# Constant row numbers, an earlier query and another bank for the keys in a four-layer graph network

## The chip, the core and the metric

The kernel runs on one core of one Trainium2 chip. The metric is device time in microseconds for one launch: 3656.0 us as the median of three runs of the kernel before (3653.54 to 3663.65). The profile below is of one profiled execution, whose span is 3611.7 us.

## What is computed

Four graph layers follow each other on x (4096 x 256) with one 4096 x 4096 adjacency of zeros and ones. Each layer ends with a residual and a layer norm. The reference, cut:

```python
# layer 0: mean over neighbours, then a linear layer
deg = adj.sum(1); agg = adj @ x / max(deg, 1); y = relu(concat([x, agg]) @ W + b)
# layer 1: two steps; R = row-normalised (adj + I), A = sparse attention
for n in range(2):
    q = Xa @ W1.T @ W2.T; k = Xa @ W3.T
    A = top_p(softmax(q @ k.T), 0.9)      # keep the largest until 0.9 of the mass, renormalise
    Xf = R @ Xf; Xa = A @ Xa
    Z = Z + Xf @ U1[n].T + Xa @ U2[n].T
y = layernorm(X + Z) * g + b
# layer 2: neighbours, and one number per node from the diagonal of adj @ adj
y = concat([x, adj @ x, diag(adj @ adj)]) @ weight + bias
# layer 3: symmetric normalisation with degree ** -0.5
y = relu((d[:, None] * (adj + I) * d[None, :]) @ x @ W + b)
```

## The kernel before

The 4096 rows are cut into NT = 32 tiles of 128 rows. The work is written as one stream for a framework that assigns the queues: each instruction belongs to a fixed engine, and the framework orders the instructions of an engine by their place in the program and by a model of when they are ready. An instruction can so stand in its engine's queue well ahead of the tile that it serves. All semaphores come from the framework. A tile of memory with `bufs=4` has four places in turn, and writing the fifth waits until the readers of the first are done. [...] `mm_bank` and `acc_bank` are one bank each, of which `half("mm")` and `half("acc")` hand out the two halves in turn.

**Layer 0** (12 to 485 us). `l0_main(it)` loads the adjacency of a tile in four pieces of 512 KB (L129, issued by GpSimd, four buffers), multiplies each with x in two fp32r halves (L160), casts each piece to bytes on ScalarE for later (L234), writes it to `adj8_d`, and adds it into `sums` on VectorE (L239 to L244). `l0_degrees(it-1)` makes from `sums` the degree, the reciprocals `rdeg` and `rs`, and `dinv`, the degree to the power −0.5, by one GpSimd instruction a tile (L259). `l0_end(it-1)` applies the linear layer (L274, into a half of `mm_bank`) and the layer norm. `l0_keys(it-2)` turns a finished row tile by TensorE (L170), copies it to SBUF as `xt` (L172, ScalarE), multiplies it with W3 into the other half of `mm_bank` (L201), and splits the result into an upper part (L194, `upk`, VectorE; L203, ScalarE) and a rest (L204, VectorE), which go to `kS`, the keys.

**Layer 1** has two steps. In each, iteration i of `run_step` works on three tiles at once: logits of tile i+2 in eight chunks (L358, copied out by L359), the choice of the largest entries of tile i+1 (cd), and the products of tile i. `pieces` runs through the eight chunks g = 0 to 7; after chunk g it calls the operations that `run_step` has registered with `at(g, f)`. The order of the work is thus the order of the `at` calls and their groups. Step 0 takes the 16 largest entries of a row: MAX8 over groups (L377), two FIND_INDEX8 (L474), gathers of rows by GpSimd (L616, 8 buffers G), diagonal weights (L701, `dg`), and matmuls (L703). Beside it run the product with adj (L632; adjacency bytes cast by L629) and, for the diagonal, L638. Step 1 keeps all entries above a threshold in place: MATCH_REPLACE8 (L602) and four masked products (L607) on VectorE, then transposes and matmuls over all chunks (L686, L711).

Rows that the choice can't settle are marked `bad`. `flag` counts them by two small matmuls (L536, L537), works out each row's place in a list (`slot` L542, `at` L543), writes the row numbers (`ids`, L544), and scatters the row numbers to those places in DRAM (L550, GpSimd, `list_d`). The places and row numbers are tiles of four buffers each. Late tiles of such rows are read back from the list (L801, L803) and done again.

`query` makes the query of tile i+3: it turns the rows (L170, L172), multiplies (L338, into a half of `mm_bank`), and splits the product like the keys (L194, L341 on ScalarE, L342 on VectorE). It is registered in group 6 in both steps. `mix` (L764, L766 for `h`, and in step 0 L772) multiplies the outcome of the tile before with U1 and U2, in groups 1 and 2, also by way of `mm_bank`.

**Layers 2 and 3** (3030 us to the end) are again products with the adjacency (L160) with linear layers and norms. `dinv` is used there first.

Of the kernel before, what the change touches and what calls it, by code (L numbers as in the profile page):

```python
# [12 lines left out]
I32 = mybir.dt.int32  # L13
# [35 lines left out]
def gnn_stack(ctx, tc, x, adjt, adjn, w0, b0, w1, w2t, w3t, u1t, u2t, ln_g, ln_b, w2, b2, w3, b3, out):  # L49
# [114 lines left out]
    def transposed(*srcs):  # L164

        n = 2 * len(srcs)
        ps = ps_tr.tile([P, 4, P], F32, tag="tr", name="tr")
        for s, src in enumerate(srcs):
            for c in range(2):
                nc.tensor.transpose(ps[:, 2 * s + c, :], src[:, c * P : (c + 1) * P], ident)  # L170
        t = work.tile([P, 4, P], F32, tag="xt", name="xt")
        nc.scalar.copy(t[:, :n, :], ps[:, :n, :])  # L172
        return t
# [22 lines left out]

    def make_keys(xt, dst):

        ps = half("mm")
        for c in range(2):  # L200
            nc.tensor.matmul(ps[:, :P], w3t_sb[:, c, :], xt[:, c, :], start=(c == 0), stop=(c == 1))  # L201
        up = upper(ps[:, :P])
        nc.scalar.copy(dst[:DA, :], up[:DA, :])  # L203
        nc.vector.tensor_sub(dst[DA:, :], ps[DA:, :P], up[DA:, :])  # L204


    with tc.tile_pool(name="l0", bufs=1) as l0, tc.tile_pool(name="l0w", bufs=2) as l0w:
# [14 lines left out]
        for h in range(2):  # L222
            nc.scalar.dma_start(w3t_sb[:, :, h * DA : (h + 1) * DA], w3t.rearrange("(c p) o -> p c o", p=P))
        x1 = xpool.tile([P, NT, D], F32, tag="X", name="x1")

        def l0_main(it):
            acc = ps_acc.tile([P, 512], F32, tag=("acc", "nef")[it % 2], name="acc")
# [21 lines left out]
        def l0_degrees(it, sums):  # L249
            pd = half("acc")  # L250
            nc.tensor.matmul(pd[:, 0:1], sums[:, :P], ones_col, start=True, stop=True)
            deg = pd[:, 0:1]
            rd = work.tile([P, 1], F32, tag="rdeg", name="rdeg")
            nc.vector.tensor_scalar(rd, deg, 1.0, None, op0=ALU.max)
            nc.vector.reciprocal(rd, rd)
            d1 = work.tile([P, 1], F32, tag="deg1", name="deg1")
            nc.vector.tensor_scalar(d1, deg, 1.0, None, op0=ALU.add)
            nc.vector.reciprocal(rs[:, it : it + 1], d1)
            nc.gpsimd.tensor_tensor(dinv[:, it : it + 1], d1, mhalf, op=ALU.pow)  # L259
            return rd  # L260

        def l0_agg(acc, rd):
# [5 lines left out]
        def l0_end(it, agg):  # L268
            xi = l0w.tile([P, D], F32, tag="x0i", name="x0i")
            nc.scalar.dma_start(xi, rows(x, it))  # L270
            xt = transposed(xi, agg)
            ps = half("mm")
            for c in range(4):
                nc.tensor.matmul(ps, xt[:, c, :], w0_sb[:, c, :], start=(c == 0), stop=(c == 3))  # L274
# [12 lines left out]

        acc = None
        for it in range(NT + 2):
            if 1 <= it <= NT:  # L290
                agg = l0_agg(acc, l0_degrees(it - 1, sums))
            if it < NT:
                acc, sums = l0_main(it)
            if it >= 2:
                l0_keys(it - 2)
            if 1 <= it <= NT:
                l0_end(it - 1, agg)


    with tc.tile_pool(name="l1", bufs=1, reuse_waits="tile") as l1:  # L300
# [20 lines left out]
        nc.vector.memset(spare0, 0.0)  # L321
        blank = l1.tile([P, NT], I32, name="blank")
        nc.gpsimd.iota(blank, pattern=[[0, NT]], base=N, channel_multiplier=1)
        for t in list_d:
            nc.sync.dma_start(t[:N, :].rearrange("(k p) o -> p (k o)", p=P), blank)

# [3 lines left out]
                nc.scalar.dma_start(t, src[n].rearrange("(c p) o -> p c o", p=P))  # L330
                cur[name] = t

        def query(xi):

            xt = transposed(xi)
            ps = half("mm")
            for c in range(2):
                nc.tensor.matmul(ps[:, :P], wq_sb[:, c, :], xt[:, c, :], start=(c == 0), stop=(c == 1))  # L338
            up = upper(ps[:, :P])
            q = [work.tile([P, P], F32R, tag=f"q{k}", name=f"q{k}", bufs=3) for k in range(2)]  # L340
            nc.scalar.copy(q[0], up)  # L341
            nc.vector.tensor_sub(q[1], ps[:, :P], up)  # L342
            return q
# [182 lines left out]
        def flag(st):  # L526


            pb = half("mm")
            later = st.get("later")  # L530
            if later is None:
                nc.tensor.matmul(pb[:1, 0:1], st["bad"], ones_col, start=True, stop=True)
                st["nb"] = small("nbad", 1, I32)[:1, :]
                nc.scalar.copy(st["nb"], pb[:1, :1])
                return
            nc.tensor.matmul(pb[:, 0:1], ones_sq, st["bad"], start=True, stop=True)  # L536
            nc.tensor.matmul(pb[:, 1:2], before, st["bad"], start=True, stop=True)  # L537
            sofar, slot = small("sofar"), small("slot")
            nc.vector.tensor_add(sofar, later["base"], pb[:, 0:1])

            at, ids = small("at", 1, I32, 4), small("ids", 1, I32, 4)
            nc.vector.scalar_tensor_tensor(slot, pb[:, 1:2], later["base"], spare, op0=ALU.add, op1=ALU.subtract)  # L542
            nc.vector.scalar_tensor_tensor(at, slot, st["bad"], spare, op0=ALU.mult, op1=ALU.add)  # L543
            nc.vector.tensor_scalar(ids, spare, float(st["tile"] * P - N), None, op0=ALU.add)  # L544
            later["base"] = sofar
            if st["tile"] == NT - 1:

                st["to"] = to = small("to_last", 1, I32, 1)
                nc.vector.scalar_tensor_tensor(to, st["bad"], float(P), ids, op0=ALU.mult, op1=ALU.add)
            nc.gpsimd.indirect_dma_start(  # L550
                out=list_d[cur["n"]], out_offset=bass.IndirectOffsetOnAxis(ap=at[:, 0:1], axis=0), in_=ids, in_offset=None)

        def bit_by_bit(st):

# [302 lines left out]
        def run_step(n, es):  # L857
# [31 lines left out]
            for i in range(-2, NT):  # L889
# [18 lines left out]
                for g, fs in zip((1, 2), last):  # L908
                    for f in fs:
                        at(g, f)  # L910
                if cd is not None:
                    peak_groups(cd)
                    at(1, exp_rows, cd)
# [189 lines left out]
```

## The time and the profile before

| from the profile page | value |
|---|---|
| span | 3611.7 us |
| PE busy | 3114.6 us, 86% |
| PEld (weight loads) busy | 2528.6 us, 70% |
| DVE (VectorE) busy | 2364.5 us, 65% |
| ACT (ScalarE) busy | 1464.9 us, 41% |
| POOL (GpSimd) busy | 1005.1 us, 28% |
| mean granted TensorE clock | 0.935 |
| L544 `ids`, DVE, x64 | 9.3 us, 150 ns each |
| L259 `dinv`, POOL, x32 | 18.1 us, 566 ns each |
| scatter to `list_d`, issue to landing | 8.3 us median |
| gathers G, issue to landing | 4.4 us median |

A share of busy time is a mean over stages that have different limits, so the stages have to be read one by one. A matmul's end is modelled in the records, so a busy PE may still be slower than it could be: the granted clock, 1.0 or 0.5, says by how much. A wait is put down to what released it last; only waits of the engine that sets the end of its stage cost time.

### The profile page before, as it was taken

Reading aid. Unit: us, or ns where it says so; the run is one execution under the profiler, and the core shown is the slowest. Engines: PE = TensorE matmul, PEld = TensorE weight load, DVE = VectorE, ACT = ScalarE, POOL = GpSimd, SP = SyncE. Lnnn points to the kernel's source line nnn. Section 1 sums busy time; section 2 is a strip of 40 time slices with the busy share of each in tenths; the row PEclk is TensorE's granted clock in tenths of the full one; section 3 lists DMA queues with packets and bytes.
Section 4 is the critical chain, followed back from the end, with each engine's and each line's share of the span. In section 5 each row is a group of like instructions: output and inputs, shape, how many; then the busy total and the mean of one; then the engine's idle time right before and its main releaser. Section 6 shows DMA issues by size and latency. Waiting matters only on the chain. (4 is left out here: it accounts for less than half of the span.)

```text
span 3611.7 us, 46113 instructions
## 1 busy us (share of the span) xinstructions
PE 3114.6 (86%) x14780; PEld 2528.6 (70%) x14780; DVE 2364.5 (65%) x7144; ACT 1464.9 (41%) x2590; POOL 1005.1 (28%) x1328
## 2 busy tenths in 40 slices
PE   7777857898899899868898989999999737999998
PEld 5666645777777777646777777777788625887776
DVE  5566545776767777734688889799889673434333
ACT  3343334554545555444544545555465301111000
POOL 1222203666666666610000000100101012222332
PEclk8999978999999999988999999999999868999999
DMA  7777665676667767723000012011111007887887
GB/s 225 207 217 210 203 93 155 156 178 171 170 163 179 176 176 177 177 86 116 28 23 23 26 31 40 24 31 34 34 33 33 17 19 231 246 246 241 269 271 227
DMA packets 269343, 484.19 MB, mean 134 GB/s; under 512 B 44096, under 2 KB 186240, under 8 KB 269088
## 3 DMA queue, kind: packets, MB, share of 16 engines
q0 software_dynamic: 101760, 339.45, 34.5%
q1 hardware_dynamic: 150352, 125.73, 12.7%
q10 hardware_dynamic: 16976, 15.95, 1.5%
q8 instruction: 120, 1.97, 0.2%
q14 instruction: 135, 1.11, 0.1%
HBM read 423.45 MB, written 57.54 MB: 133 GB/s over the span
## 5 line engine op out<-in xcount | busy, mean ns | idle before, releaser
L632 PE MATMUL acc_r<-xh,adjq 128*128 128x512 f32 x2048 | 639.3, 444 | 49.1 <-ACT adjq L629 36.8
L616 POOL DMA_INDIRECT G<-x_d,cols x512 | 496.3, 969 | 355.1 <-PE acc_bank L703 262.9
L711 PE MATMUL acc_bank<-xa,at 128*128 128x256 f32 x2304 | 569.5, 387 | 18.0 <-ACT at L689 17.5
L160 PE MATMUL acc<-xh,adjt 128*128 128x512 f32 x2048 | 544.3, 416 | 45.4 <-DVE xh L137 29.4
L632 PEld LDWEIGHTS acc_r<-xh,adjq 128*128 128x128 f32 x2048 | 395.2, 199 | 152.8 <-ACT adjq L629 61.4
L358 PE MATMUL lg<-kS,q 128*128 128x512 f32 x1104 | 407.8, 456 | 97.7 <-ACT q L341 83.7
L160 PEld LDWEIGHTS acc<-xh,adjt 128*128 128x128 f32 x2048 | 391.8, 196 | 136.2 <-ACT xh L136 31.2
L711 PEld LDWEIGHTS acc_bank<-xa,at 128*128 128x128 f32 x2304 | 424.5, 194 | 80.1 <-ACT at L689 28.9
L629 ACT CAST adjq<-adj 128x512 fp32r<-128x512 uint8 x512 | 315.3, 619 | 387.3 <-issue 128.4
L377 DVE MAX8 cand<-e 128x8 f32<-128x256 f32 x1024 | 384.0, 415 | 40.1 <-ACT e L359 39.0
L129 POOL DMA_DIRECT2D adjt<-in_adjt x384 | 208.6, 544 | 695.4 <-PE acc L160 392.9
L359 ACT COPY e<-lg 128x512 f32<-128x512 f32 x552 | 317.8, 584 | 166.9 <-PE lg L358 164.8
L184 POOL TENSOR_TENSOR rstd<-ve,mhalf 128x1 f32<-128x1 f32 x168 | 102.7, 611 | 800.4 <-DVE ve L182 747.9
L703 PE MATMUL acc_bank<-G,dg 128*128 128x256 f32 x1024 | 292.6, 403 | 16.3 <-DMA G<-x_d,cols 11.0
L474 DVE FIND_INDEX8 cols<-top,e 128x8 uint32<-128x4096 f32 x64 | 282.8, 4419 | 0.0
L358 PEld LDWEIGHTS lg<-kS,q 128*128 128x128 f32 x1104 | 190.7, 199 | 124.9 <-ACT q L341 90.2
L160 PE MATMUL acc<-yh,adjt 128*128 128x512 f32 x1024 | 256.0, 402 | 2.5 <-DMA adjt<-in_adjt 2.1
L234 ACT CAST a<-adjt 128x1024 uint8<-128x1024 f32 x128 | 133.9, 1046 | 271.8 <-DMA adjt<-in_adjt 128.3
L689 ACT COPY at<-at_ps 128x512 f32<-128x512 f32 x296 | 172.4, 589 | 175.9 <-PE at_ps L686 175.4
L703 PEld LDWEIGHTS acc_bank<-G,dg 128*128 128x128 f32 x1024 | 201.5, 200 | 58.1 <-DMA G<-x_d,cols 11.3
L160 PEld LDWEIGHTS acc<-yh,adjt 128*128 128x128 f32 x1024 | 190.0, 188 | 47.2 <-DMA adjt<-in_adjt 2.8
L686 PE MATMUL at_ps<-ident,e 128*128 128x128 f32 x1184 | 184.3, 279 | 40.9 <-DVE e L607 25.3
(270 smaller groups left out, 4515.5 us busy)
## 6 DMA issues: line engine op xcount, KB each, us to landing
adjt<-in_adjt POOLq DMA_DIRECT2D x384, 512.0 KB, 5.0
adjn<-in_adjn POOLq DMA_DIRECT2D x128, 512.0 KB, 5.6
adj<-adj_d SPq DMA_DIRECT2D x256, 128.0 KB, 3.0
adj_d<-a SPq DMA_DIRECT2D x128, 128.0 KB, 3.9
x_d<-x SPq DMA_DIRECT2D x64, 128.0 KB, 4.9
xf_d<-xf_new SPq DMA_DIRECT2D x64, 128.0 KB, 2.9
G<-x_d,cols POOLq DMA_INDIRECT x512, 4.4
xf<-xf_d SPq DMA_DIRECT2D x64, 128.0 KB, 2.0
```

The costliest lines, as they stand in the source:

```text
L129: nc.gpsimd.dma_start(t, src[it, :, c * jp : (c + 1) * jp, :])
L160: nc.tensor.matmul(acc, a[:, j, :], halves(jt), start=(jt == 0), stop=(jt == NT - 1))
L358: nc.tensor.matmul(pl[:, :LC], q[k], kS[:, s], start=(k == 0), stop=(k == 1))
L359: nc.scalar.copy(l[:, s], pl[:, :LC])
L377: nc.vector.max(dst[:, 8 * g : 8 * g + 8], src[:, g * GW : (g + 1) * GW])
L474: nc.vector.max_index(st["at"][:, 8 * r : 8 * r + 8], t8, st["e"][:, :N])
L616: nc.gpsimd.indirect_dma_start(out=g, out_offset=None, in_=x1_d, in_offset=bass.IndirectOffsetOnAxis(ap=st["at"][:, k : k + 1], axis=0))
L629: nc.scalar.copy(a, cur["a8"][:, g % 2 * GP : (g % 2 + 1) * GP, :])
L632: nc.tensor.matmul(acc_r, a[:, j, :], xf[:, jt, :], start=(jt == 0), stop=False)
L686: nc.tensor.transpose(ps[:, j, :], e[:, (g * G + j) * P : (g * G + j + 1) * P], ident)
L703: nc.tensor.matmul(acc_a, dg[:, k % 4, :], st["G"][k], start=(k == 0), stop=(k == KEPT - 1))
L711: nc.tensor.matmul(acc_a, ats[g][:, j, :], cur["xa"][:, jt, :], start=(jt == 0), stop=(jt == NT - 1))
```

## The change

The diff has four parts. The row numbers of all tiles become one constant tile, `ids` [128 x 32], written once at the start of layer 1; the list places `at` become columns of two tiles, `slots_of`, one for each step; L544 goes away. The query is cut in two: the turning of the rows (`transposed`) is registered one group ahead of the matmul and the split, in groups 5 and 6 in step 0, and in groups 0 and 1 in step 1, where all of it was in group 6 before. In layer 0 the keys of a tile are made three tiles behind rather than two, and their matmul goes to a rotating bank of the pool that the logits use later, not to `mm_bank`. And the degrees plus one are kept in a tile `deg1`, of which one GpSimd instruction takes all powers after the loop. What it is for: engines should not stand in line for buffers and banks that they don't need.

```diff
     def make_keys(xt, dst):
-        ps = half("mm")
+        ps = ps_lg.tile([P, 512], F32, tag="lg", name="k_ps")
         for c in range(2):
             nc.tensor.matmul(ps[:, :P], w3t_sb[:, c, :], xt[:, c, :], start=(c == 0), stop=(c == 1))
...
+        deg1 = l0.tile([P, NT], F32, name="deg1")
...
-            d1 = work.tile([P, 1], F32, tag="deg1", name="deg1")
+            d1 = deg1[:, it : it + 1]
             nc.vector.tensor_scalar(d1, deg, 1.0, None, op0=ALU.add)
             nc.vector.reciprocal(rs[:, it : it + 1], d1)
-            nc.gpsimd.tensor_tensor(dinv[:, it : it + 1], d1, mhalf, op=ALU.pow)
...
-        for it in range(NT + 2):
-            if 1 <= it <= NT:
+        for it in range(NT + 1):
+            if it >= 1:
                 agg = l0_agg(acc, l0_degrees(it - 1, sums))
             if it < NT:
                 acc, sums = l0_main(it)
-            if it >= 2:
-                l0_keys(it - 2)
-            if 1 <= it <= NT:
+            if it >= 3:
+                l0_keys(it - 3)
+            if it >= 1:
                 l0_end(it - 1, agg)
+        nc.gpsimd.tensor_tensor(dinv, deg1, mhalf.to_broadcast([P, NT]), op=ALU.pow)
+        l0_keys(NT - 2)
+        l0_keys(NT - 1)
...
+        ids = l1.tile([P, NT], I32, name="ids")
+        nc.gpsimd.iota(ids, pattern=[[P, NT]], base=0, channel_multiplier=1)
+        slots_of = [l1.tile([P, NT], I32, name=f"slots{n}") for n in range(STEPS)]
...
-        def query(xi):
-            xt = transposed(xi)
+        def query(xi, xt=None):
+            if xt is None:
+                xt = transposed(xi)
             ps = half("mm")
...
-            at, ids = small("at", 1, I32, 4), small("ids", 1, I32, 4)
+            i = st["tile"]
+            at, rows_i = slots_of[cur["n"]][:, i : i + 1], ids[:, i : i + 1]
             nc.vector.scalar_tensor_tensor(slot, pb[:, 1:2], later["base"], spare, op0=ALU.add, op1=ALU.subtract)
             nc.vector.scalar_tensor_tensor(at, slot, st["bad"], spare, op0=ALU.mult, op1=ALU.add)
-            nc.vector.tensor_scalar(ids, spare, float(st["tile"] * P - N), None, op0=ALU.add)
...
             nc.gpsimd.indirect_dma_start(
-                out=list_d[cur["n"]], out_offset=bass.IndirectOffsetOnAxis(ap=at[:, 0:1], axis=0), in_=ids, in_offset=None)
+                out=list_d[cur["n"]], out_offset=bass.IndirectOffsetOnAxis(ap=at, axis=0), in_=rows_i, in_offset=None)
...
                 for g, fs in zip((1, 2), last):
                     for f in fs:
                         at(g, f)
+                if 0 < i + 2 < NT - 1:
+                    turned = []
+                    g = 1 if n else 6
+                    at(g - 1, lambda i, turned: turned.append(transposed(cur["xa"][:, i + 3, :])), i, turned)
+                    at(g, lambda turned: cur["qs"].append(query(None, turned[0])), turned)
...
-                if 0 < i + 2 < NT - 1:
-                    at(6, lambda i: cur["qs"].append(query(cur["xa"][:, i + 3, :])), i)
```

More of the change, by code (lines that the diff above doesn't have):

```diff
@@ L539, in flag @@
             nc.vector.tensor_add(sofar, later["base"], pb[:, 0:1])
-            at, ids = small("at", 1, I32, 4), small("ids", 1, I32, 4)
+            i = st["tile"]
+            at, rows_i = slots_of[cur["n"]][:, i : i + 1], ids[:, i : i + 1]
             nc.vector.scalar_tensor_tensor(slot, pb[:, 1:2], later["base"], spare, op0=ALU.add, op1=ALU.subtract)
             nc.vector.scalar_tensor_tensor(at, slot, st["bad"], spare, op0=ALU.mult, op1=ALU.add)
-            nc.vector.tensor_scalar(ids, spare, float(st["tile"] * P - N), None, op0=ALU.add)
             later["base"] = sofar
-            if st["tile"] == NT - 1:
+            if i == NT - 1:
                 st["to"] = to = small("to_last", 1, I32, 1)
-                nc.vector.scalar_tensor_tensor(to, st["bad"], float(P), ids, op0=ALU.mult, op1=ALU.add)
+                nc.vector.scalar_tensor_tensor(to, st["bad"], float(P), rows_i, op0=ALU.mult, op1=ALU.add)
             nc.gpsimd.indirect_dma_start(
-                out=list_d[cur["n"]], out_offset=bass.IndirectOffsetOnAxis(ap=at[:, 0:1], axis=0), in_=ids, in_offset=None)
+                out=list_d[cur["n"]], out_offset=bass.IndirectOffsetOnAxis(ap=at, axis=0), in_=rows_i, in_offset=None)
         def bit_by_bit(st):
```

## The prediction

> **What bounds the kernel now.** I read three views. First the busy time by stretch of the span, with the borders put where the stages change; columns are length, then busy time (and instruction count) of PE, PEld, DVE, ACT and POOL, then granted TensorE clock, DMA share and GB/s.
>
> ```profile
> 12.00:485.00 473.00, 374.41 (x1633) 289.19 (x1634) 282.67 (x728) 181.40 (x261) 102.83 (x186) 0.94 0.70 207
> 485.00:650.00 165.00, 106.67 (x471) 83.75 (x471) 85.00 (x247) 67.28 (x124) 47.60 (x61) 0.78 0.59 113
> 650.00:1600.00 950.00, 837.49 (x4120) 691.65 (x4120) 659.86 (x1988) 475.41 (x929) 565.37 (x624) 0.94 0.68 168
> ...
> 1720.00:2830.00 1110.00, 1032.46 (x5163) 854.26 (x5163) 947.95 (x3181) 581.68 (x971) 89.14 (x105) 0.97 0.12 30
> ...
> 3030.00:3611.00 581.00, 567.83 (x2540) 456.69 (x2538) 218.77 (x603) 65.94 (x157) 167.25 (x308) 0.99 0.81 250
> ```
>
> The rows are layer 0, the start of step 0, step 0 proper, step 1, and layers 2 and 3. In the last one PE is busy 98% at clock 0.99. In the first and third it is busy 79% and 88% at clock 0.94. No other engine is fuller, and the DMA engines there are at 0.70 and 0.68 while the last stage holds 0.81. So those two stages are TensorE stages with holes, and the question is who makes the holes. Second, the waits, for step 0 (650 to 1600), for layer 0 (12 to 485), and for step 1 (1720 to 2830): who waited for whom, total us, times, longest.
>
> ```profile
> DVE ids L544 <- DMA list_d<-ids,at: 203.0, 28, 9.7
> PE lg L358 <- ACT q L341: 61.2, 27, 4.8
> ```
> ```profile
> PE mm_bank L274 <- DVE kS L204: 46.3, 28, 2.8
> PE mm_bank L201 <- ACT xt L172: 42.2, 29, 4.9
> ```
> ```profile
> PE lg L358 <- ACT q L341: 22.2, 8, 4.7
> PE mm_bank L536 <- DVE bad L508: 19.2, 14, 3.5
> ```
>
> Step 0 has the largest: VectorE stands 7.25 us (203.0/28) in nearly every tile at L544, the writing of a tile of row numbers. Third, the timeline of one tile of step 0, POOL, DVE, ACT and PE in turn (start, length, engine, instruction, then the idle time ahead of it).
>
> ```profile
> 1012.04 1.00 POOL L550 DMA_INDIRECT list_d<-ids,at  x1 [0.30 <-issue]
> ```
> ```profile
> 1011.49 0.67 DVE L701 TENSOR_TENSOR dg<-ident,w 128x512 f32<-128x512 f32 x1
> 1020.47 0.15 DVE L544 TENSOR_SCALAR ids<-spare 128x1 int32<-128x1 f32 x1 [8.31 <-DMA list_d<-ids,at]
> 1020.54 1.07 DVE L377 MAX8 cand<-e 128x8 f32<-128x256 f32 x3
> 1021.53 0.27 DVE L194 TENSOR_SCALAR upk<-mm_bank 128x128 int32<-128x128 int32 x1
> ```
> ```profile
> 1021.84 0.30 ACT L341 CAST q<-upk 128x128 fp32r<-128x128 f32 x1 [4.10 <-DVE upk L194]
> ```
> ```profile
> 1018.21 0.56 PE L638 MATMUL nef_ps<-adjn,adjq 128*128 128x128 f32 x4
> 1022.19 1.22 PE L358 MATMUL lg<-kS,q 128*128 128x512 f32 x2 [3.42 <-ACT q L341]
> 1023.21 1.91 PE L703 MATMUL acc_bank<-G,dg 128*128 128x256 f32 x4
> 1024.55 2.27 PE L632 MATMUL acc_r<-xh,adjq 128*128 128x512 f32 x4
> ```
>
> The scatter is issued at 1012.04 and lands a median of 8.3 us later: 1020.4, when L544 runs. So L544 is writing the row numbers of a later tile, pulled ahead in the queue and waiting for one of its four buffers, which this scatter is still reading. Behind it stand three MAX8 and `upk`, the split of the next query; behind that the cast, and behind that the first logits of the next tile. PE gets 3.42 us of nothing, then half speed: four L632 take 2.27 us here and 1.28 elsewhere (the clock of 1022 to 1026 is 0.50).
>
> [...] half speed after the 3.42 us gap. So a hole costs more than its length. [...] L274 writes one half of `mm_bank` and still waits until L204 has read the other half. [...]
>
> **Row numbers and places as constants.** Removes 64 L544 of 0.15 us (9.3 us of DVE in all) and its waits (269.8 us, 42 times, over the whole trace). The new `ids` is written once by POOL. `at` goes into its own column, so it never waits for a buffer. Work: two `iota`-like POOL writes of a few us at most, beside the layer 0 to step 0 change-over; zero.
>
> **Step 0.** With the wait gone `upk` can run about when its matmul ends (L338, 1016.8), `q` by 1017.8, before PE ends its tile at 1018.8. Putting transposes and matmul in separate groups (5 and 6) takes the copy `xt` off that path too. Gain one: the 61.2 us. Gain two: the lost clock, (1−0.94)×950 = 57 us, of which I give three quarters to this gap[...]: 43. Sum 104; I take 100. Does something else end last? The tile is 31.5 us long (L634, once a tile, starts at 681.7 first and at 1594.6 as the thirtieth; so 950 us are 30.2 tiles) and would be about 31.5 − 100/30.2 = 28.2. POOL needs 16 gathers × (0.97+0.30) + 4 loads × 0.60 + a scatter 1.3 = 24.0 us; DVE 659.86/30.2 = 21.9; ACT 15.7; the DMA share becomes 0.68×31.5/28.2 = 0.76, under the 0.81 that the last stage holds. All fit.
>
> **Layer 0.** The keys' matmul moves from `mm_bank` to a rotating bank that layer 0 does not otherwise use. L274 then needs only its own `xt`, copied before (both copies of L172 come together). Gain: 46.3 us. The clock there loses 0.06×473 = 28 us; half of the PE waiting goes, so I take 16. The 42.2 us of L201 on `xt` I leave: the copy stands in ACT's queue behind the cast L234, which waits for a load (115.9 us of such waits between 100 and 480), and having the keys three tiles behind makes the input ready earlier but not that queue. It is the upper end, +42. Limit: 207 GB/s × 473 us = 97.9 MB, at the last stage's 250 GB/s 392 us, so at most 81 us can come out of layer 0. Taken: 62.
>
> **Degree powers.** Takes 32 POOL instructions of 0.57 us (18.1 us, and 88.2 us of POOL waiting for DVE) out of the queue that issues the loads of `adjt`; the next load waited for PE afterwards anyway, so zero by itself. The one power on 128x32 is not in the trace: at least 0.57 us, at most 32 × 0.57 = 18 us if it costs per column. Only loads of the start of step 0 can be behind it; I take 3 us lost, with the two last keys now behind the loop.
>
> **Step 1.** Query in groups 0 and 1 rather than 6: `upk` no longer sits behind the 4.4 us MATCH_REPLACE8 and four 1.28 us products. Gain: 22.2 us[...]. Against it: L338 now follows the mix L764 in the same bank, so PE must wait until DVE has read `h` (L766), which in two tiles I looked at ran 0.2 to 0.6 us after the mix ended; PE has other matmuls to put between, so 0 to 1.3 us × 30 tiles. Net +15. **Start of step 0:** logits wait 9.4 us for `q` once and L544 17.4 us; +8.
>
> Sum: 100+62−3+15+8 = 182, hence 3656−182 = 3474.
>
> **Rivals.** (a) Half: with the tile shorter, PE meets the next things in line: G rows landing 4.4 us after issue from a POOL that is 24.0 us full of 28.2, and in layer 0 the loads[...]. Then half of 100 and of 62 and nothing of step 1: 50+30+5 = 85, 3571. For: POOL runs without a break from 1012 to 1022. Against: it has some 7 us free in the first half of a tile. (b) More: the wait of L201 and all clock loss go: 61+57+81+36+8 = 243, 3413. For: three-behind keys have their input a whole tile early. (c) Slower: a wait on a PE or POOL result takes L544's place on DVE (it waits for L537 already, 35.1 us in step 0), step 0 and layer 0 gain nothing, and the query behind the mix costs PE 1.5 us in each of 30 tiles: 3656+45 = 3701. For: every engine order shifts with the edit. Against: the removed wait has no twin; nothing in the new code reuses a buffer that a scatter reads.
>
> **Chances.** Main 0.60, (a) 0.18, (b) 0.12, (c) 0.10, of which 0.08 slower and 0.02 within 0.3%. The range 3400 to 3590 holds the first three with the bounds of the power (15 us) and of the step 1 wait (39 us), and leaves out (c).
>
> **What would show it.** Right: no L544 and no DVE wait on `list_d` but that of `from`; PE on ACT `q` near zero in step 0, its clock above 0.98, tile about 28 us; L274 without waits on `kS`. Wrong: PE waits on G or `adjn`, or L338 on L766, in their place; or the clock stays at 0.94, which would say that the hole was filled by another.

## The result and the profile after

The kernel after takes 3634.16 us (median of four runs, 3632.0 to 3639.99) where the kernel before took 3656.97 beside it: a ratio of 0.9938, with a 95% interval of 0.992 to 0.9956. It is faster, by 23 us and not by the 182 us forecast, and the time lies above the range. The profiled execution of before took 3613.5 us, less than any of the four timed ones beside the kernel after (3653.54 to 3663.65), so the two profiles' spans (3611.7 and 3632.9 us) stand the other way round; the change is therefore read from stages and waits, and both kernels are profiled once more below.

The same view of busy time by stretch as in the prediction, now of the kernel after (length, then PE, PEld, DVE, ACT and POOL, then granted clock, DMA share, GB/s):

```profile
12.00:485.00 473.00, 391.54 (x1682) 311.94 (x1683) 284.21 (x755) 183.81 (x272) 92.48 (x164) 0.90 0.69 209
650.00:1600.00 950.00, 817.83 (x4009) 682.12 (x4008) 652.63 (x1876) 464.64 (x897) 557.31 (x616) 0.92 0.69 165
1720.00:2830.00 1110.00, 1036.43 (x5210) 853.48 (x5208) 949.18 (x3159) 594.46 (x990) 84.64 (x104) 0.98 0.13 31
```

The clock of step 0 was to rise above 0.98; it is 0.92 here (0.94 before), and 0.94 in both kernels when they are profiled again (650 to 1580). That of layer 0 was to rise too and fell from 0.94 to 0.90. Now TensorE's waits in step 0 (650 to 1600) and in layer 0 (12 to 485):

```profile
PE nef_ps L646 <- DMA adjn<-in_adjn: 82.5, 26, 5.1
PE acc_r L640 <- DVE xh L137: 9.9, 3, 8.0
```
```profile
PE k_ps L201 <- ACT xt L172: 60.4, 29, 3.4
PE mm_bank L274 <- ACT xt L172: 7.1, 2, 6.4
```

Both waits that the change was aimed at are gone: no logits wait for `q` in step 0, and L274 waits for no `kS`. In their places stand two others. In step 0, TensorE waits as often as before (26 times, 27 before), but for a load of the adjacency, `adjn`, in the product for the diagonal (L646, L638 before): 82.5 us here where it waited 61.2 for `q`, and 64.8 against 67.5 when both are profiled again. In layer 0 the keys' matmul waits for the copy `xt` 60.4 us, where it was 42.2. The timeline of a tile of step 0 shows how (start, length, engine, instruction, the idle time ahead of it):

```profile
1015.07 1.00 POOL L558 DMA_INDIRECT list_d<-ids,slots  x1 [0.30 <-issue]
...
1018.59 0.60 POOL L129 DMA_DIRECT2D adjn<-in_adjn  x1
...
1018.81 0.29 DVE L194 TENSOR_SCALAR upk<-mm_bank 128x128 int32<-128x128 int32 x1 [1.17 <-PE mm_bank L346]
1019.14 0.30 ACT L349 CAST q<-upk 128x128 fp32r<-128x128 f32 x1 [0.16 <-issue]
...
1022.69 1.28 PE L640 MATMUL acc_r<-xh,adjq 128*128 128x512 f32 x4
1028.89 1.09 PE L646 MATMUL nef_ps<-adjn,adjq 128*128 128x128 f32 x4 [4.92 <-DMA adjn<-in_adjn]
```

`upk` and `q` follow their matmul at once, as predicted, 3.7 us after the scatter was issued and without waiting for it. The scatter goes out at 1015.07, and a load issued behind it at 1018.59 is still missing at 1024; TensorE can use it at 1028.89, 10.3 us after its issue, where the median landing of such loads is 5.6 us in before. TensorE stands 4.92 us and then runs at half speed: four L646 take 1.09 us here and 0.56 otherwise. The hole has only changed its name.

What the loads wait for is seen when the stretches are cut to 2 us. First the kernel before, around its scatter at 1012.04, then the kernel after, around 1015.07 (columns as above; the last two are DMA share and GB/s):

```profile
1014.00:1016.00 2.00, 2.00 (x13) 1.58 (x11) 0.00 (x0) 0.87 (x3) 1.69 (x3) 1.00 0.87 117
1016.00:1018.00 2.00, 2.00 (x12) 1.70 (x12) 0.00 (x0) 0.98 (x3) 1.39 (x3) 1.00 0.97 35
...
1022.00:1024.00 2.00, 1.81 (x4) 1.50 (x5) 2.00 (x11) 1.29 (x3) 0.00 (x0) 0.50 0.93 319
1024.00:1026.00 2.00, 2.00 (x6) 1.57 (x5) 2.00 (x4) 2.00 (x5) 1.16 (x2) 0.50 1.01 374
```
```profile
1018.00:1020.00 2.00, 2.00 (x14) 1.81 (x14) 0.58 (x2) 1.31 (x3) 1.69 (x3) 1.00 1.78 70
1020.00:1022.00 2.00, 2.00 (x12) 1.71 (x11) 1.77 (x7) 1.15 (x3) 1.43 (x2) 1.00 0.39 35
1022.00:1024.00 2.00, 1.97 (x9) 1.32 (x7) 0.51 (x3) 1.24 (x2) 1.66 (x2) 1.00 0.59 47
...
1028.00:1030.00 2.00, 1.11 (x5) 1.14 (x6) 1.90 (x3) 1.01 (x2) 0.95 (x1) 0.50 1.08 404
```

In both kernels there is a stretch of some 6 to 8 us behind the scatter in which the DMA engines are busy by their records and move 35 to 117 GB/s, and after it one in which they make up for it at 319 to 404 GB/s. It is so behind all of them: over the 28 scatters from 650 to 1500 in before, the four stretches of 2 us from 2 to 10 us after the issue carry 50, 39, 49 and 60 GB/s in the mean, over the 27 in the kernel after 40, 30, 49 and 37 (packets counted where they end). (A share over 1 comes from a packet's whole time being booked where it starts.) The share of 0.87 at 117 GB/s and that of 0.93 at 319 look alike; only the bytes tell them apart. The mean of the stage, 0.68, hid a stop in nearly every tile.

### The profile page after: what moved, and what is told of

Its sections match the earlier page's. It is cut to its first block, busy times and chain, and to the rows that moved or that the text cites. A ratio compares the mean times of both kernels' runs of the same rounds, so it can differ in the third digit from the quotient of the medians.

```text
span 3632.9 us, 46132 instructions
## 1 busy us (share of the span) xinstructions
PE 3122.7 (86%) x14780; PEld 2543.5 (70%) x14780; DVE 2368.7 (65%) x7080; ACT 1472.3 (41%) x2590; POOL 987.0 (27%) x1298
## 5 line engine op out<-in xcount | busy, mean ns | idle before, releaser
L640 PE MATMUL acc_r<-xh,adjq 128*128 128x512 f32 x2048 | 629.5, 439 | 74.6 <-ACT adjq L637 53.0
L160 PE MATMUL acc<-xh,adjt 128*128 128x512 f32 x2048 | 535.7, 414 | 45.5 <-ACT xh L136 24.3
L646 PEld LDWEIGHTS nef_ps<-adjn,adjq 128*128 128x128 f32 x1024 | 161.2, 205 | 128.8 <-issue 80.2
L646 PE MATMUL nef_ps<-adjn,adjq 128*128 128x128 f32 x1024 | 158.8, 280 | 96.7 <-DMA adjn<-in_adjn 96.6
```

The lines of the kernel that those rows point to most:

```text
L160: nc.tensor.matmul(acc, a[:, j, :], halves(jt), start=(jt == 0), stop=(jt == NT - 1))
L640: nc.tensor.matmul(acc_r, a[:, j, :], xf[:, jt, :], start=(jt == 0), stop=False)
L646: nc.tensor.matmul(pn[:, :P], a[:, j, :], cur["b"][:, jt % (2 * GP), :], start=(jt == 0), stop=(jt == NT - 1))
```

## The experiments

### What stops: the scatter, GpSimd or the buffers

Three theories, named A, B and C in the expectations: A, that each scatter of 128 numbers of four bytes stops all DMA transfers for some 8 us, so that L544 was only the first to stand in line for it; B, that GpSimd, 24 us full of each tile, issues the loads too late; C, that places for `adjn` or others come free too late. The experiments were run in groups, each group on one chip. The first holds the kernel before again, and the kernel after with its scatters left out, doubled, and spread. In the one without scatters all but that of the last tile of each step are left out, so that rows that were put off stay as they are:

```diff
+            if i == NT - 1:
-            nc.gpsimd.indirect_dma_start(
+                nc.gpsimd.indirect_dma_start(
```

For the doubled one the same statement stands there twice. The spread one writes the same numbers at places 512 bytes apart instead of four, and so does the fill of the lists with row numbers ahead of step 0 (L332, 4096 numbers for each list):

```diff
-    list_d = [dram.tile([N + P, 1], I32, name=f"list{n}_d") for n in range(STEPS)]
+    list_d = [dram.tile([N + P, 128], I32, name=f"list{n}_d") for n in range(STEPS)]
...
-            nc.sync.dma_start(t[:N, :].rearrange("(k p) o -> p (k o)", p=P), blank)
+            nc.sync.dma_start(t[:N, 0:1].rearrange("(k p) o -> p (k o)", p=P), blank)
...
+            nc.vector.tensor_scalar(at, at, float(128), None, op0=ALU.mult)
...
-                out=list_d[cur["n"]], out_offset=...
+                out=list_d[cur["n"]].rearrange("a (b o) -> (a b) o", o=1), out_offset=...
...
-            nc.sync.dma_start(to, list_d[n][slots, :])
+            nc.sync.dma_start(to, list_d[n][slots, 0:1])
```

> The kernel before, unchanged, for a profile on the same chip as the runs beside it: the profile shown before the prediction is of an execution of 3613.5 us, 1.2% under the median of 3657. If the profiles can be compared as they are, this one has about 3613 us and step 0 of some 866 us (from the first to the last product for the diagonal); if that one execution was a lucky one, 3650 to 3665, and step 0 is where the 40 us lie.

> The changed kernel without the scatters of row numbers, except that of the last tile of each step (so rows that are put off stay as they are: that part of the output is left out; the late tiles run as long as before). Theory A, the scatter of 128 numbers of four bytes keeps all 16 DMA engines from moving data for some 8 us, and the adjn load that ends the wait of TensorE stands behind it: the 82.5 us of waits for adjn in step 0 go and with them half of the lost clock, so about 3634-80-40 = 3515. Theory B, GpSimd's queue is full and the adjn load is issued late: the scatter costs only its 1.3 us of the queue, 31 x 1.3 = 40 us at the most, 3595 to 3630. Theory C, two buffers for adjn are too few for the shorter tile: no change, 3625 to 3635.

> The changed kernel with each scatter issued twice, with the same data. Theory A: another 7 to 8 us without data in each of some 28 tiles of step 0, and the tile is already waiting for it: +150 to +210, 3785 to 3845. Theory B: 1.3 us more of GpSimd's queue in a tile: +40, 3675. Theory C: 3634 to 3645.

> The changed kernel with the list spread out: each four-byte number goes to a row of 512 bytes of its own, where before the 128 numbers of a tile went to neighbouring places, 512 bytes together (one more small VectorE instruction multiplies the places). Theory A in the form that the writes hinder each other at one place: the stall goes, 3515 to 3560. Theory A in the form that a four-byte write is slow wherever it goes: no change, 3630 to 3645. Theories B and C: no change, 3630 to 3645.

| kernel | ratio to before [95%] | last key of layer 0, us | step 0 from there, us | step 1, us |
|---|---|---|---|---|
| before again | (3619.5 us) | 502 | 1012 | 1128 |
| no scatter | 0.9458 [0.9429, 0.9487] | 480 | 909 | 1060 |
| two scatters | 1.0713 [1.0681, 1.0744] | 482 | 1266 | 1136 |
| spread | 0.9408 [0.9384, 0.9433] | 488 | 887 | 1062 |

(Step 0 is counted from the last key to the last matmul into `nef_ps`; step 1 from the last transposed key to the last product with the adjacency. The kernel after was not run in this group; in the second, on another chip, it has 0.9908, and 484, 1014 and 1111.) TensorE's waits on `adjn` from 650 to 1500 in the kernel after, with two scatters, and spread:

```profile
PE nef_ps L646 <- DMA adjn<-in_adjn: 79.3, 25, 5.1
```
```profile
PE nef_ps L648 <- DMA adjn<-in_adjn: 228.1, 21, 13.9
```
```profile
PE nef_ps L647 <- DMA adjn<-in_adjn: 1.7, 2, 1.2
```

And the stretch 650 to 1500 of the spread kernel, followed by that of the kernel after:

```profile
650.00:1500.00 850.00, 791.08 (x4088) 661.79 (x4087) 645.67 (x1893) 470.13 (x911) 547.24 (x594) 0.98 0.61 182
```
```profile
650.00:1500.00 850.00, 754.51 (x3749) 634.01 (x3748) 599.08 (x1748) 431.01 (x837) 508.58 (x567) 0.93 0.70 167
```

The spread kernel gets 4088 matmuls done in the time of 3749, at clock 0.98, moves more bytes (182 GB/s against 167), and its DMA engines are *less* busy: 0.61 against 0.70. (The kernel after of the second group has 3855 matmuls, 0.95, 173 GB/s and 0.71.) The rows of issues, with the time to landing at the end, agree; they are of before, two scatters and spread:

```profile
list_d<-ids,at POOLq DMA_INDIRECT x64, 8.3
```
```profile
list_d<-ids,slots POOLq DMA_INDIRECT x128, 8.5
```
```profile
list_d<-ids,slots POOLq DMA_INDIRECT x64, 2.5
```

A holds, and it answers to the dose. A second scatter adds 252 us to step 0 (1266 − 1014), 7.9 us for each of its 32, nearly all of its 8.5 us. Taking the first away brings 105 (1014 − 909), 3.4 us for each of 31; that loads made ahead cover the rest of its stop is likely, but not measured. These figures set two chips side by side, and between chips step 0 of one kernel has differed by 65 us (below); on the chip of 1266 and 909 the kernel before has 1012. The regular tiles say the same: from one tile's first product for the diagonal to the next tile's, the median is 30.7 us in before again, 30.6 in after, 39.5 with two scatters, and 27.2 both without scatters and spread. In size A had asked too little each time: 3515 us without scatters, 3785 to 3845 with two and 3515 to 3560 spread were expected, and 3425, 3872 and 3403 came. B and C fall with the spread kernel: GpSimd issues the same instructions there and the buffers are the same, and the wait is gone. Nor are four-byte writes as such slow: the 128 writes of the spread kernel are as many and as small, and land 2.5 us after their issue. The 8.3 and 8.5 us go with neighbouring places. In the packets of the trace it is seen too: of some 31,900 packets of 4096 bytes in step 0, those that took over 1 us are 884 in before again, 245 in spread and 1721 with two scatters.

The spread kernel is also shorter than the one without scatters, by 22 us in step 0 (887 and 909), though the regular tiles are the same. Seventeen of these lie at the start of step 0: from the last key to the first product for the diagonal it takes 37.1 us in before again and without scatters, and 19.6 spread. The second changed line of the edit is the likely cause, the fill of the lists, which is four-byte writes to neighbouring places as well. Without scatters, but with that fill, the DMA engines move 15 to 38 GB/s from 480 to 496, and TensorE then waits for a cast of the adjacency; first without scatters, then in the spread kernel, where it waits less (both from 478 to 520):

```profile
PE acc_r L641 <- ACT adjq L638: 29.1, 1, 29.1
```
```profile
PE acc_r L641 <- ACT adjq L638: 12.3, 2, 11.6
```

SyncE issues the fill, and it isn't indirect. So neither GpSimd's queue nor the indirect form would be what matters; but no run spreads the fill alone. In all kernels with spread lists this start takes 19 to 22 us, in all others 35 to 42.

How far apart they must be, and whether the place of the cure matters, was asked with the places 64 bytes apart, with the spread list put into the kernel before and nothing else, and with all parts but the query. "Spread" in the second and third of these is 512 bytes; the 64-byte list and a repeat of the 512-byte one are the whole kernel after.

> The kernel before with the constant row numbers, the layer 0 parts and the spread list, the query left where it was: the change without its query part, with the list that no longer holds up the DMA engines. Spread on the whole change gave 0.941 of before. If the query in two parts costs by itself (alone it gave 1.015, 26 us of it in step 1), this is faster than that: 0.930 to 0.938. If the query part only did harm by being in line with the wait at the row numbers or behind the scatter, both gone here: 0.938 to 0.946.

> The kernel before with the spread list alone; row numbers, query and layer 0 as they were. Theory A: the wait at the row numbers was one of several things that stood behind the scatter; it shrinks from 7 us a tile to 1 or 2 with the scatter's landing (2.5 us in place of 8.3), so nearly the whole gain comes without the change: step 0 890 to 910 us (1012 before), step 1 1065 to 1085 (1128 before), 0.950 to 0.955. If the row numbers as constants are needed beside it: 0.97.

> The changed kernel with the list spread out less: each number in a row of 64 bytes of its own (512 before). If the four-byte writes hinder each other only within 64 bytes: as with 512, 3400, 0.941. If a neighbour within 512 bytes still hinders: the landing of the scatter between 2.5 and 8.3 us and the time between 3400 and 3597. If what counts is that all lie in few neighbouring rows: 3590.

> The changed kernel with the list in rows of 512 bytes, as once before (0.941, step 0 887 us, every tile 27.2 us). If that was the kernel and not the chip: 0.938 to 0.944 again and tiles of 27.2 us. If the chip of the later runs is what made tiles of 28 to 31 us: 0.950 to 0.957.

> The changed kernel with rows of 64 bytes, on the same chip as rows of 512. If a neighbour within 512 bytes still hinders: 1.5 to 2% slower than with 512 bytes, as in the two runs on different chips. If 64 bytes are enough: the same within 0.4%.

> The kernel before with constants, layer 0 parts and rows of 512 bytes, the query left in one part and in group 6, on the same chip as the two before. If the query part is worth its gain once the scatter is out of the way: step 0 40 to 70 us longer than with it (930 to 957 us), 1.5 to 2% slower. If that difference was the chip: equal within 0.4%.

| kernel (group) | ratio to before [95%] | step 0, us | step 1, us |
|---|---|---|---|
| spread 512, all but the query (3) | 0.9561 [0.9536, 0.9586] | 957 | 1058 |
| before + spread 512 (3) | 0.9606 [0.9575, 0.9637] | 956 | 1061 |
| after + spread 64 (3) | 0.9539 [0.951, 0.9568] | 944 | 1062 |
| after + spread 512 (4) | 0.9546 [0.9515, 0.9577] | 952 | 1062 |
| after + spread 64 (4) | 0.9542 [0.951, 0.9575] | 953 | 1062 |
| spread 512, all but the query (4) | 0.9574 [0.9543, 0.9604] | 972 | 1059 |

64 bytes are as good as 512 (0.9542 and 0.9546, each known to 0.3%); less was not tried. With the query's split, which had nothing to give before, step 0 is 20 us shorter in the profiles (972 to 952), but the intervals of the two ratios overlap, so that this gain isn't shown. The spread list alone, in the kernel before with its L544 and its four buffers, brings 4%; VectorE's wait at L544 shrinks there to this in step 0 (203.0 us in before):

```profile
DVE ids L544 <- DMA list_d<-ids,at: 33.4, 21, 3.6
```

So the wait at L544 didn't need another buffer; it needed the transfer to end sooner. One thing here stays open: the same kernel, after with 512 bytes, had 0.9408 and a step 0 of 887 us in the first group, and 0.9546 and 952 us in the fourth, on another chip (kernels of one group ran on one chip). The regular tiles take 27.2 us there and 28.3 to 29.5 in the later groups. The ratios within a group don't suffer from it, but the size of the gain differed by more than one per cent from group to group, with the chip as the one known difference, and no run says why. Expectations that took the first group's 0.941 as given missed for it: 0.941 for 64 bytes (0.9539 came), 0.930 to 0.946 for all but the query (0.9561), and 0.950 to 0.955 with a step 0 of 890 to 910 us for the spread list alone (0.9606 and 956).

### The parts one by one

The second group has the kernel after again and its parts alone, each put into the kernel before: the constants and list places; layer 0 with the degree powers; the query.

> The changed kernel, unchanged, with more rounds, beside its parts and on a chip whose runs of before can be compared with those of the profile. Theory A: the wait that is removed from VectorE comes back as a wait of TensorE for adjn, so 0.99 to 1.00 of before, what remains being layer 0.

> The kernel before with the constant row numbers and places alone. By the prediction: -100, 0.972 of before. Theory A (the DMA engines stand after each scatter): TensorE waits for the adjn load where it waited for the query, 0.995 to 1.005 of before.

> The kernel before with the layer 0 parts alone (keys in another bank and three tiles behind, the powers at once). By the prediction: -59, 0.984. By the two profiles, in which the last key of layer 0 comes 20 us earlier and the wait of the keys' matmul for its input grew from 42 to 60 us: -15 to -20, 0.995.

> The kernel before with the query in two parts alone. By the prediction: step 0 gains next to nothing while VectorE still stands at the row numbers, step 1 gains 15: 0.996. By the two profiles, in which step 1 got 14 us shorter: the same, 0.996. If the query placed behind the mix hinders TensorE in step 1: 1.005 or more.

| kernel | ratio to before [95%] | last key | step 0 | step 1 |
|---|---|---|---|---|
| after | 0.9908 [0.9887, 0.9929] | 484 | 1014 | 1111 |
| constants alone | 0.99 [0.9879, 0.9921] | 503 | 1013 | 1094 |
| layer 0 alone | 0.9969 [0.9958, 0.998] | 478 | 1015 | 1127 |
| query alone | 1.0148 [1.0124, 1.0173] | 506 | 1040 | 1154 |

(before, on the chip of the first group: 502, 1012, 1128; the profile of layer 0 alone is of the shortest of its ten executions, 3597.66 us where the median is 3619.74.) The stages agree with the times of this group: the constants alone take 39 us off, 34 of them in step 1; the kernel after takes 33 off, 18 in layer 0 and 17 in step 1. So the constants brought nothing in step 0, for which they were forecast, and 34 us in step 1, for which the prediction had not counted them. In step 0 TensorE waits for `adjn` there too, 42.3 us in 22 pieces (650 to 1580), where the kernel before waited for `q`. The query alone costs 1.5% where +15 us of gain stood in the sum. With the early query L544 still stands in front of `upk`, so that its loss could have come from their meeting. Therefore two last kernels, in a fifth group on the chip of the second; they are the kernel after, where L544 is gone: the query of step 1 put back into group 6, and that of step 0.

```diff
-                if 0 < i + 2 < NT - 1:
+                if 0 < i + 2 < NT - 1 and n == 0:
                     turned = []
...
+                if 0 < i + 2 < NT - 1 and n == 1:
+                    at(6, lambda i: cur["qs"].append(query(cur["xa"][:, i + 3, :])), i)
```

> The kernel after with the query of step 1 put back into group 6, in one piece; step 0 keeps the query in groups 5 and 6. If the early query of step 1, ahead of the mix in groups 1 and 2, is what costs there, step 1 goes from 1111 (after, profile of the second call) to about 1094 us, the length with the constants alone, and the ratio falls from 0.991 to about 0.986. If step 1 does not care, its length stays within 5 us of that of after and the ratio is the same. The prediction's own theory, a gain of 15 us from the early query, expects step 1 15 us longer here than in after, ratio 0.995.

> The kernel after with the query of step 0 put back into group 6, in one piece; step 1 keeps the query in groups 0 and 1. If the split in step 0 costs TensorE in the presence of the scatters as the query alone seemed to show (28 us in step 0), step 0 gets 10 to 28 us shorter than in after (1014), ratio 0.983 to 0.988. If the stall behind each scatter sets the length of step 0 whatever the order, step 0 stays within 10 us of 1014 and the ratio at 0.991.

Early in step 0 alone: 0.9819 [0.98, 0.9838], step 0 1005 us, step 1 1093. Early in step 1 alone: 0.9926 [0.9912, 0.9939], 1015 and 1117. The early place in step 1 costs some 20 us, with L544 (1154 against 1128) or without (1111 and 1117 against 1093). The split in step 0 is worth about nothing while the stall sets that stage (1005 with it, 1015 without, 1014 in the kernel after, which has it too). Three rows of TensorE's waits in step 1, first with the query in group 6, then three with the early one (1720 to 2800):

```profile
PE acc_bank L719 <- ACT at L697: 24.2, 14, 5.4
PE at_ps L694 <- issue: 14.0, 1, 14.0
PE lg L366 <- ACT q L349: 5.1, 1, 5.1
```
```profile
PE acc_bank L719 <- ACT at L697: 32.2, 17, 6.6
PE mm_bank L772 <- ACT xt L172: 9.0, 2, 6.2
PE acc_r L640 <- ACT adjq L637: 8.7, 4, 4.9
```

With L544 gone, the query in group 6 makes TensorE wait 5.1 us once; there were 22.2 us in before. So there was nothing left for the early place to gain. What it seems to do instead: ScalarE has the copy and the split of the query in its queue early in the tile, ahead of the copies `at` and the casts `adjq`, and TensorE waits longer for these (32.2 and 8.7 us, where `at` alone took 24.2). That the order on ScalarE is the cause is read from these rows and was not tested. Over the whole of step 1 TensorE is idle 73 us of 1116 with it and 58 of 1093 without, the busy time differing by 8. With the spread list the early query showed no such loss (1062 us against 1059), so which copies stand in line depends on more than this edit; that was not followed further.

### Layer 0

TensorE's wait moved from `kS` to `xt`. In the profile ScalarE, which makes `xt`, waits itself (12 to 485, kernel after):

```profile
ACT a L235 <- DMA adj_d<-a: 147.0, 58, 4.8
ACT a L235 <- DMA adjt<-in_adjt: 115.1, 37, 6.8
```

The first, for the store of adjacency bytes out of one of two places, was 51.6 us in before again (12 to 470). So: four places for `a8`, and besides, the keys' rows turned and copied a whole tile ahead of their matmul, into a tile of their own.

```diff
-                a8 = l0w.tile([P, JP, P], U8, tag="a8", name="a8")
+                a8 = l0w.tile([P, JP, P], U8, tag="a8", name="a8", bufs=4)
...
-            make_keys(transposed(x1[:, it, :]), kS[:, it * P : (it + 1) * P])
+            make_keys(turned.pop(it), kS[:, it * P : (it + 1) * P])
...
             if it >= 3:
                 l0_keys(it - 3)
+            if it >= 2:
+                l0_turn(it - 2)
```

> The changed kernel with four buffers for the byte copies of the adjacency in layer 0 (two before). In the changed kernel ScalarE waits 147 us there for the store of such a copy (45 before), and the input copy that TensorE waits for (59.9 us) stands behind it. If that is why layer 0 gave 18 us and not 62: layer 0 ends 30 to 45 us earlier (438 to 453 for its last keys, 484 without), 0.980. If TensorE's wait is for the loads that the cast needs: layer 0 unchanged within 5 us, 0.991.

> The changed kernel with rows of 512 bytes, four buffers for the byte copies in layer 0, and the keys' input turned and copied a tile ahead of the keys' matmul. If TensorE's 60 us wait for that copy is what layer 0 lost: its last key at 430 to 445 us (488 with the rows of 512 bytes alone), 40 to 55 us less in all than the first run of this call. If the loads set layer 0 and the wait only showed it: 465 to 475, 15 less, the part of the four buffers.

Four places alone, in the kernel after: 0.9851 [0.982, 0.9881], last key at 470 us, where 438 to 453 were expected if the store was what layer 0 lost. With the turning ahead as well and the spread list of 512 bytes: 0.9462 [0.9435, 0.949], last key at 447 us; beside 484 us and 0.9546 for the kernel with the spread list alone, that is 31 us less time (3441.06 against 3471.87, same group), between the 15 and the 40 to 55 of the two expectations. It was the shortest of its group. The stretch 12 to 445 without and with these two:

```profile
12.00:445.00 433.00, 358.91 (x1530) 285.28 (x1531) 260.38 (x684) 169.51 (x244) 81.05 (x148) 0.90 0.72 217
```
```profile
12.00:445.00 433.00, 368.00 (x1663) 291.13 (x1662) 279.72 (x748) 182.00 (x265) 91.25 (x162) 0.96 0.74 228
```

1663 matmuls in place of 1530 take hardly more busy time, and the clock is 0.96 and not 0.90. TensorE's waits in that stretch, without and with:

```profile
PE k_ps L201 <- ACT xt L172: 56.8, 27, 3.5
```
```profile
PE mm_bank L274 <- ACT xt L172: 38.8, 29, 2.7
PE ktr L290 <- DVE x L189: 16.9, 20, 4.3
```

The sum of these rows is the same (56.8 and 55.7 us), but in 49 pieces and not in 27: a mean of 1.1 us instead of 2.1. Shorter stops go with a higher clock here (0.96 at a mean of 1.1 us, 0.90 at 2.1). But the clock alone doesn't account for the gain: in thirteen profiles with the layer 0 of the kernel after it lies anywhere from 0.88 to 0.93 in this stretch, and the matmuls done only from 1510 to 1552. How much came from each of the two edits was not separated. With four places alone ScalarE's wait for the store only became one for the loads (199.4 us on `adjt` from 12 to 445), so most of its 147 us were no loss of their own; 14 us were (484 to 470, on two chips).

## Why the prediction was wrong

**Step 0, −100 us.** Measured: 1012 to 1014 us, no gain. The mechanism that the prediction read in its timeline, scatter, L544, `upk`, `q`, logits, was there, and the change removed it: no logits wait for `q`. The tile was to shrink from 31.5 to 28.2 us; its median went from 30.7 to 30.6. The step that failed is "Does something else end last?", and in it the sentence "the DMA share becomes 0.68×31.5/28.2 = 0.76, under the 0.81 that the last stage holds. All fit." It took a busy DMA engine for one that moves bytes. Behind the scatter at 1012.04 the share was 0.87 and 0.97 at 117 and 35 GB/s. The load of the next piece of `adjn` stands behind the scatter as L544 did; TensorE needs it only a little later than it had needed `q`, and in the kernel before it had landed by the time the wait for `q` was over: TensorE waits 0.7 us for `adjn` in that stage. TensorE runs at half speed after the new hole as it did after the old one: four L646 take 1.09 us behind 4.92 us without work (0.56 otherwise), as four L632 took 2.27 us behind 3.42 us (1.28 elsewhere). So the clock term fell with the wait: one hole in place of another is one loss of clock in place of another (0.94 in both kernels from 650 to 1580, when profiled again). That this hole held three quarters of the lost clock, 43 us, was the author's estimate and was not shown. The 182 us of the whole sum are not far from what the scatters cost in the kernel after (some 163 us: 0.9908 − 0.9458 of 3618, from two groups; 105 of them in step 0 and 51 in step 1), which is luck: the edits of the sum took away a symptom.

**The rivals.** "What would show it" named the right sign of being wrong: "PE waits on G or `adjn` … in their place", or a clock that stays at 0.94, "which would say that the hole was filled by another". Both came. Rival (a) looked for the next in line too, but in step 0 it named G and put it down to GpSimd being full, and gave half the gain. The runs show no gain there, a wait on `adjn`, and GpSimd without a part in it. (b) supposed less waiting on L201, and there was more. (c) was right that step 0 gains nothing, for another reason than its own: it looked for a wait of VectorE in the place of L544, and though VectorE does wait for TensorE more (75.1 us at `dg` from 650 to 1580, 5.7 in before), TensorE itself stands for a load. It was also right that the earlier query costs TensorE in step 1, about 20 us where it said 45.

**Layer 0, −62 us.** Measured −18 (502 to 484). The 46.3 us of L274 on `kS` are gone, as worked out; the bank and the place of the keys were changed together, and no run parts them. Two terms failed. L201's wait, left at 42.2, became 60.4: the two stops of a tile, 1.7 and 1.5 us in the mean, became one of 2.1. And the clock, put at +16 us, did not come back but went from 0.94 to 0.90. With −46 for L274 and +18 for L201, 28 us would be left, and 18 came; how much of the other 10 is the clock stays open. By the prediction's arithmetic 0.04 of 433 us would be 17 us, but among kernels with this layer 0 the clock ranged over 0.05 and the last key, leaving out layer 0 alone, only from 480 to 488 us. That longer stops go with a lower clock is supported by the kernel with the turning ahead, where about the same waiting in shorter stops goes with 0.96; four places alone left the stops as they were (54.3 us, 28 times) and the clock at 0.91.

**Degree powers, +3 us.** One instruction on 128x32 took 5.43 us (row below), between the bounds of 0.57 and 18, and layer 0 alone shows no stage that it made clearly longer (478 and 1015). That it cost nothing is the reading of whole stages, not a separate run.

```profile
L298 POOL TENSOR_TENSOR dinv<-deg,mhalf 128x32 f32<-128x32 f32 x1 | 5.4, 5432 | 4.3 <-DVE deg L258 4.3
```

**Step 1, −15 us.** The sign of the query's part was wrong: it costs about 20. A part of its +15 was an estimate of clock to be won back, which was not shown. The 22.2 us of logits waiting for `q` were counted for the early place, and they belonged to L544, which the constants remove (4.9 us are left with the constants alone); the same wait was paid for twice over. What the prediction left out, that removing L544 helps step 1 as well, is 34 us (1128 to 1094). The net, 1128 to 1111, is 17 us, near the 15 forecast, by luck: one term has the wrong sign and the other was not in the sum. **Start of step 0, −8:** from the last key to the first product for the diagonal it takes 37.1 us in before again and 35.5 in after again, so 2 us at most; the fill of the lists, which the prediction did not look at, is likely what takes 17 of them.

**The range.** It reached to half the gain, since it took the wait in step 0 for at least half removable. The chance of "nothing in step 0" was given only together with "nothing in layer 0", in (c).

## What to carry to other kernels

When an engine waits for a transfer, ask first why the transfer takes so long, and only then who else could wait: take the bytes per us and the busy share of the DMA engines in stretches of 2 us around it, and where the share stays up and the bytes are few, as here at 0.97 and 35 GB/s, suspect that a transfer holds up all others, and that another place to write only hands the wait on, as the constants alone did (42.3 us of TensorE on `adjn` from 650 to 1580, where before again waits 67.5 for `q`). Spreading or leaving out that transfer tests it. Before removing a wait, look for what else was issued behind the same event, and count a wait once if two edits would remove it. Small results that are scattered to memory are worth trying at places 64 bytes apart: in the kernel after that did as well as 512 (0.9542 and 0.9546), and 512, together with the fill of the lists, cost one multiplication a tile and brought 4% in the kernel before, where all of the change brought 0.9%.

## What was not expected of the hardware

A scatter of 128 numbers of four bytes into neighbouring places takes 8.3 us from issue to landing (median, before), and in the four stretches of 2 us from 2 to 10 us behind its issue all transfers together get 39 to 60 GB/s in before and 30 to 49 in after (means of 28 and 27 scatters). Into places 512 bytes apart it took 2.5 us, the same stretches got 110 to 288 GB/s in the mean of 28 scatters, and TensorE waited only 1.7 us for `adjn` from 650 to 1500, where it had waited 79.3. Places 64 bytes apart gave the same times: 0.9542 of before against 0.9546, and a step 0 of 953 us against 952. So the size of a write alone isn't what counts here: the same four-byte writes leave the stage as short when each has 64 bytes for itself, eight to a stretch of 512, as when each has all 512. Why neighbouring writes take longer no run shows. The second is a difference between groups that ran on two chips: the same spread kernel differed by 1.4% of the time of before, nearly all of it in step 0 (887 and 952 us).
